# Rows of the first three chunks gathered ahead of the branch, in a graph network kernel on one core

## The chip, the core and the metric

The kernel runs on one core of a Trainium2 chip. The metric is the device time of one execution in microseconds, as the median over several runs. A core has five engines with instruction streams of their own, each of which runs in order: PE (matrix products and transposes), DVE (element-wise work and reductions), ACT (activations and copies), POOL (here almost only the issue of indirect transfers) and SP (here only the issue of plain transfers). PEld stands for PE's loading of its fixed operand. Transfers between the chip's memory and the on-chip buffers are done by 16 DMA engines.

## What is computed

Two graph attention layers with a batch normalisation between them, over 6250 nodes of 128 features and 106,250 edges that are sorted by target node, then a residual and a layer normalisation. Cut to what matters:

```python
def _transformer_conv(h, edge_attr, src, dst, Wq, bq, Wk, bk, Wv, bv, We, Ws, bs):
    q, k, v = ...                        # h @ W + b, as (n, H=2, 64)
    e = (edge_attr @ We).reshape(-1, H, C)
    kj = k[src] + e
    alpha = jnp.einsum('ehc,ehc->eh', q[dst], kj) / sqrt(C)
    a = ...                              # softmax of alpha over the edges of one dst
    out = segment_sum((v[src] + e) * a[:, :, None], dst, num_segments=n)
    return out.reshape(n, H * C) + h @ Ws + bs

rel_t = last_update[src] - t             # node_vec[src] - edge_weight
edge_attr = concatenate([cos(rel_t[:, None] * time_w + time_b), msg], -1)   # 32 + 64 columns
h = _transformer_conv(x, edge_attr, ...)
h = relu(batchnorm(h))
out = layernorm(x + _transformer_conv(h, edge_attr, ...))
```

For each edge the features of its source node are needed, in the first layer also one number of that node, its time, from which 32 cosines of the edge are made.

## The kernel before, in words

**The plan.** The first part (L1429 to L1607) runs ahead of a branch. It loads the sources, the targets and the weights of the edges as 104 rows of 1024 and turns them into columns (`columns`: `fsrcs` at the start, `fdsts` later, `few`, the edge weights, as the last thing): 8 columns of 128 edges for each of 104 chunks. It loads `x` in four parts into `fhT`, where node times stand beside the rows as column 0 (the copies of L530), and writes this 129-column form back to memory as `xv_d`. It checks that the edges are as the fast path wants them and leaves the verdict in `oki`. It makes the matrices of the first layer (`matrices`: L583 to L604), a code matrix (`codes`: L614 to L622), and the first 512 nodes' block of a table that the scores are read from (`tables`: L630 to L642, with a skip row block). PE's results go through two rings of two PSUM banks, `fpt` (128 columns) and `fpx` (512 columns). Each engine then loads `oki` and branches, to `ordered`, or else to `general`, which is not run here.

**The fast path.** `ordered` turns the features of all nodes into columns (`turn_features`: L656 and L658, twelve groups of four transposes, whose copies alternate between DVE and ACT, and a short one, L661 and L662) and then runs `conv(0)` and `conv(1)`. Each goes over 104 chunks of 1024 edges in rounds written out by hand: in round k chunk k is scored (`score`, L954), the weights of chunk k-1 are turned (`turn_weights`, L978), chunk k+1 is turned (`turn_in`: the gathered rows by L913, the encoded edge terms by L925), chunk k+2's times become cosines (`encode`: the angle on DVE, L878 to L886, and the sine on ACT, L892), the bits of chunk k+3's targets are made (`mark`: L829 to L832), chunk k+4 is fetched, and chunk k-1's weighted rows are summed (`gather_sums`, L1001).

**The gathers.** The 1024 source rows of a chunk come by eight indirect transfers of 128 rows each, issued by POOL (`gather`, L839), in the first layer from `xv_d`, in the second from `h_d` and `hn_d`. A chunk's edge data, rows and times share one tile `ff`, from a pool of 7 in the first layer and of 6 in the second. A chunk is gathered four rounds ahead in the first layer and three in the second. Tile 0 of chunk k+4 follows the last step of an earlier `gather_sums`, tile 1 the first half of `score(k)`, tile 2 the turned weights of chunk k-1, tile 3 `finish_turn`, tiles 4 and 5 the two halves of `turn_in(k+1)`, tiles 6 and 7 the first and second third of `gather_sums(k-1)`. These are waits of POOL for PE. Rounds -4 to -2 only fetch and gather chunks 0 to 2, without such waits; chunk 3 belongs to round -1.

**The extra work.** A generator `rest()` supplies work that isn't tied to a chunk, a step at each pull, a few pulls at the end of a round: in before first `targets()` (L712 to L738, PE at L732), which gives the sums of a round their target rows, then the other blocks of the table (L630, L638), then the second layer's matrices.

The early rounds pull two steps each:

```python
pull(extra, (3 if k == 3 else 2) if c and k < 6 else 2 if k < 4 or k > 96 else 1)
```

## Time and profile before

| What | Value |
|---|---|
| Median of three runs | 2177.34 us (2177.1, 2177.34 and 2183.26) |
| Profiled execution | 2178.58 us, of which the recorded span is 2176.8 us |
| Mean granted clock of PE | 0.874 |
| Busy: PE, DVE, ACT, POOL | 1664.4, 1104.6, 972.6, 1578.6 us |
| First gather, last gather of conv 0, first of conv 1 | 33.59, 1072.41, 1106.24 us |
| Branch on PE | between 43.5 and 44.5 us |

A row of the timeline gives the start, the duration, the engine and line, what is written and read, the number of instructions put together, and in brackets how long the engine had been idle and what ended that. "issue" there means that nothing in the profile was waited for. A row of groups gives total busy time, mean time of one in ns, idle time before them and the releaser. A row of windows gives busy time in a stretch, with the clock granted to PE, the share of the DMA engines' time and GB/s at the end. Line numbers are those of the kernel before, and `f` is put in front of the tiles' names.

### The profile page before, as it was taken

Reading aid. Unit: us, or ns where it says so; the run is one execution under the profiler, and the core shown is the slowest. Engines: PE = TensorE matmul, PEld = TensorE weight load, DVE = VectorE, ACT = ScalarE, POOL = GpSimd, SP = SyncE. Lnnn points to the kernel's source line nnn. Section 1 sums busy time; section 2 is a strip of 40 time slices with the busy share of each in tenths; the row PEclk is TensorE's granted clock in tenths of the full one; section 3 lists DMA queues with packets and bytes.
Section 4 is the critical chain, followed back from the end, with each engine's and each line's share of the span. In section 5 each row is a group of like instructions: output and inputs, shape, how many; then the busy total and the mean of one; then the engine's idle time right before and its main releaser. Section 6 shows DMA issues by size and latency. Waiting matters only on the chain.

```text
span 2176.8 us, 46498 instructions
## 1 busy us (share of the span) xinstructions
PE 1664.4 (76%) x13227; PEld 984.3 (45%) x13227; DVE 1104.6 (51%) x3702; ACT 972.6 (45%) x1828; POOL 1578.6 (73%) x1684
## 2 busy tenths in 40 slices
PE   5887787877777878877867777787877778786776
PEld 3455455545455545554534434443444434443333
DVE  4866666656666666676636333333333333332223
ACT  1766666655555555566643333333332333332223
POOL 3777777777777777777557777777777777777773
PEclk9889988879999999899888888888888888888888
DMA  7777777777677777778758667676666667677662
GB/s 210 197 224 210 206 221 211 212 202 210 191 213 199 212 213 210 205 215 219 214 156 240 190 170 193 180 197 178 185 193 188 193 182 187 181 196 185 172 157 76
DMA packets 427316, 424.02 MB, mean 195 GB/s; under 512 B 297704, under 2 KB 344722, under 8 KB 423722
## 3 DMA queue, kind: packets, MB, share of 16 engines
q1 hardware_dynamic: 353086, 272.62, 44.0%
q0 software_dynamic: 53184, 109.45, 21.0%
q10 hardware_dynamic: 20780, 38.87, 5.0%
q8 instruction: 109, 1.79, 0.4%
q14 instruction: 157, 1.29, 0.2%
HBM read 274.73 MB, written 142.58 MB: 192 GB/s over the span
## 4 chain that ended last, share of the span: by engine, by line
DMA 36%; PE 34%; DVE 15%; issue 8%; POOL 4%; ACT 2%; SPq 1%; DVEq 0%; POOLq 0%; ACTq 0%
DMA ff<-hn_d,fsrcs 19%; DMA ff<-xv_d,fsrcs 11%; PE fpa L1001 9%; PE fps L954 7%; PE fpx L913 5%; POOL ff L839 4%; DVE farg L885 3%; PE fpg L630 3%; PE fpe L925 2%; PE fpa L1025 1%; DVE fa L1013 1%; PE fppt L978 1%; DVE fangles L883 1%; DVE farg L879 1%; DVE fangles L882 1%
## 5 line engine op out<-in xcount | busy, mean ns | idle before, releaser
L839 POOL DMA_INDIRECT ff<-xv_d,fsrcs x831 | 786.8, 947 | 283.1 <-issue 115.5
L839 POOL DMA_INDIRECT ff<-hn_d,fsrcs x783 | 742.5, 948 | 241.1 <-issue 105.4
L913 PE MATMUL fpx<-fident,ff 128*128 128x128 f32 x1664 | 335.8, 312 | 231.1 <-DMA ff<-hn_d,fsrcs 211.2
L1001 PE MATMUL fpa<-ff,fpt 128*32 128x256 f32 (+1 forms) x4160 | 416.2, 453 | 0.5 <-ACT fpt L979 0.4
L917 ACT COPY fft<-fpx 128x512 f32<-128x512 f32 x404 | 234.6, 581 | 354.1 <-PE fpx L913 348.8
L913 PEld LDWEIGHTS fpx<-fident,ff 128*128 128x128 f32 x1664 | 229.8, 156 | 294.8 <-DMA ff<-hn_d,fsrcs 248.8
L979 ACT COPY fpt<-fppt 128x384 f32<-128x384 f32 x208 | 99.9, 480 | 504.8 <-PE fppt L978 477.8
L954 PE MATMUL fps<-fft,ftab 128*32 128x384 f32 (+2 forms) x1782 | 264.8, 514 | 32.6 <-ACT fs L969 31.1
L1001 PEld LDWEIGHTS fpa<-ff,fpt 128*32 128x32 f32 (+1 forms) x4160 | 143.7, 129 | 272.2 <-issue 188.5
L1084 DVE TENSOR_SCALAR fout<-fres,fmean,fvar 64x128 f32<-64x128 f32 x104 | 36.7, 353 | 348.2 <-ACT fvar L1082 340.2
L1025 PE MATMUL fpa<-fsel,fa 128*128 128x128 f32 x207 | 65.1, 315 | 160.3 <-DVE fsel L1015 153.4
L925 PE MATMUL fpe<-fident,ff 128*112 128x128 f32 x832 | 153.3, 317 | 3.0 <-ACT ff L892 3.0
L962 DVE TENSOR_REDUCE flow<-fps 128x1 f32<-128x384 f32 x208 | 115.4, 555 | 77.0 <-PE fps L954 75.3
L878 DVE TENSOR_TENSOR frel<-ff,few 128x8 f32<-128x8 f32 (+1 forms) x105 | 18.2, 174 | 254.8 <-DMA ff<-xv_d,fsrcs 254.4
L926 ACT COPY fet<-fpe 112x512 f32<-112x512 f32 x208 | 123.6, 595 | 47.1 <-DMA et_d<-fet 34.1
L954 PE MATMUL fps<-fet,ftab 112*32 112x384 f32 (+3 forms) x968 | 143.0, 456 | 0.0
L885 DVE SCALAR_TENSOR_TENSOR farg<-fangles,farg 128x256 f32<-128x256 f32 (+1 forms) x315 | 132.8, 421 | 10.9
L978 PE MATMUL fppt<-fident,fs 128*128 128x128 f32 x626 | 111.7, 289 | 28.5 <-DVE fbits L829 16.7
L954 PEld LDWEIGHTS fps<-fft,ftab 128*32 128x32 f32 x1782 | 86.3, 119 | 96.4 <-ACT fs L969 44.5
L969 ACT ACTIVATE fs<-fps,fm 128x384 f32<-128x384 f32 x208 | 121.2, 583 | 7.9 <-DVE fm L964 6.9
L954 PE MATMUL fps<-fxT,ftab 112*32 112x384 f32 (+2 forms) x900 | 120.6, 492 | 3.2 <-DMA fxT<-et_d 3.0
L925 PEld LDWEIGHTS fpe<-fident,ff 128*112 128x112 f32 x832 | 120.2, 158 | 3.9 <-ACT ff L892 3.9
(247 smaller groups left out, 2421.3 us busy)
## 6 DMA issues: line engine op xcount, KB each, us to landing
ea_d<-ff SPq DMA_DIRECT2D x104, 448.0 KB
et_d<-fet SPq DMA_DIRECT2D x104, 448.0 KB
ff<-ea_d SPq DMA_DIRECT2D x104, 448.0 KB
fxT<-et_d SPq DMA_DIRECT2D x104, 448.0 KB
tab_d<-fo ACTq DMA_DIRECT2D x26, 1024.0 KB
ftab<-tab_d SPq DMA_DIRECT2D x832, 32.0 KB
ff<-in_edge_attr SPq DMA_DIRECT2D x103, 256.0 KB
ff<-xv_d,fsrcs POOLq DMA_INDIRECT x831
```

What stands on the lines that cost most here:

```text
L839: row = nc.gpsimd.indirect_dma_start(out=f[:, t, :D + 1 - c], out_offset=None, in_=(h_d[:N, :] if k < RAW else hn_d) if c else pl.xv_d, in ...
L885: nc.vector.scalar_tensor_tensor(arg, turn, -part, arg, op0=OP.mult, op1=OP.add)
L913: last = nc.tensor.transpose(px[:, t * P:(t + 1) * P], s.x[:, u * 4 + t, 1 - c:1 - c + D], ident)
L917: nc.scalar.copy(s.ft[:, u * GE:(u + 1) * GE], px)
L925: last = nc.tensor.transpose(pe[:EC, t * P:(t + 1) * P], s.e[:, u * 4 + t], ident)
L926: nc.scalar.copy(s.et[:, u * GE:(u + 1) * GE], pe[:EC])
L954: steps.append(nc.tensor.matmul(s.ps[r, to:to + n], s.tab[:kd, r, i], (ets if i else fts)[:kd, at:at + n], start=i == 0, stop=i == 1 and t ...
L962: nc.vector.tensor_reduce(low, s.ps, AX.X, OP.min)
L969: nc.scalar.activation(s.s[:, :s.ps.shape[1]], s.ps, AF.Exp, bias=s.bias, scale=-1.0)
L978: last = nc.tensor.transpose(pp[:, t * P:(t + 1) * P], s.s[:, t * P:(t + 1) * P], ident)
L979: nc.scalar.copy(s.pt[:, :n * P].rearrange("p (g t c) -> p t g c", g=NQ, c=GH), pp[:, :n * P].rearrange("p (t g c) -> p t g c", g=NQ, c=GH))
L1001: steps.append(nc.tensor.matmul(s.pa[g * GH:(g + of) * GH].rearrange("p (a d) -> p a d", a=2), s.pt[:, (g * n + t) * GH:(g * n + t + of) * ...
```

## The change

Five things change together.

1. The chunks' buffers become one tile, `fring`, of seven slots, allocated ahead of the plan and used by both layers (`split_rows`); `general` uses the same room.
2. The 24 gathers of chunks 0 to 2 move into the plan, behind the column of sources. They read rows of 128 columns from `x` itself and leave the time column free; `gather` returns at once for these chunks.
3. The time column of these chunks is filled by `pick_times`: for each half chunk (six units) one product spreads the high part of the source numbers over 49 partitions, a comparison makes a 0/1 matrix of it, four products with the times (`fhours`, 49 x 128) pick a row of 128 times for each edge, and four reductions with an equality on the low part pick one of them. The units are interleaved with `matrices` and `tables`.
4. `turn_features` leaves the place ahead of conv 0 and becomes the first part of `rest()`, ahead of `targets()`: four groups are pulled in round -1, five in round 0, and in round 1 the last three, the short one and `targets()`.
5. `hide()` in the second layer takes its buffers in turn from two pools.

```diff
+RING = 7
+EARLY = 3
...
+def split_rows(pl, slot):
+    f = pl.ring[:, slot % RING]
+    return (f, f[:, :T * EC].rearrange("p (t d) -> p t d", d=EC),
+            f[:, T * EC:].rearrange("p (t d) -> p t d", d=1 + D))
+
+def pick_times(nc, pl, pool, bank, srows, node_vec):
...
+    for k in range(EARLY):
+        times = split_rows(pl, k)[2]
+        for u in range(T // 4):
+            pb = bank()
+            nc.tensor.matmul(pb[:NA], one[:, k], hi[:, u * GE:(u + 1) * GE], start=True, stop=True)
+            oh = pool.tile([NA, GE], F32, name="foh", bufs=2)
+            nc.vector.tensor_scalar(oh, pb[:NA], lane[:NA], None, op0=OP.is_equal)
+            yield
+            pc = bank().rearrange("p (i n) -> p i n", n=P)
+            for i in range(4):
+                nc.tensor.matmul(pc[:, i], oh[:, i * P:(i + 1) * P], pl.hours, start=True, stop=True)
+            for i in range(4):
+                t = u * 4 + i
+                junk = pool.tile([P, P], F32, name="fjunk", bufs=2)
+                nc.vector.scalar_tensor_tensor(junk, pl.place_of, lo[:, t, k:k + 1], pc[:, i], op0=OP.is_equal,
+                                               op1=OP.mult, accum_out=times[:, t, 0:1])
+            yield
...
-            s.f = load.tile([P, T * FW], F32, name="ff")
...
+            s.f, s.e, s.x = split_rows(pl, k + c * NC)
...
         def gather(k, rows, behind=None):
             f = ch[k].x
+            if c == 0 and k < EARLY:
+                return
...
-                step = put_rows(hn_d, b0, *turned_rows(b0, small.tile([P, GE // P, P], F32, name="fhn", bufs=4)))
+                rows = small.tile([P, GE // P, P], F32, name="fhn", bufs=2) if b0 % 2 else None
+                step = put_rows(hn_d, b0, *turned_rows(b0, rows))
...
+                if c == 0 and k in (-1, 0, 1):
+                    pull(extra, 4 if k < 0 else 2)
...
-                        pull(extra, (3 if k == 3 else 2) if c and k < 6 else 2 if k < 4 or k > 96 else 1)
+                        pull(extra, (3 if k == 3 else 2) if c and k < 6 else 1 if k < 0 else 3 if k < 4 else 2 if k == 4 or k > 96 else 1)
...
-            turn_features(nc, pl, mp, N)
...
             others = second()
+            yield from turn_features(nc, pl, lambda: pl.bank(), N)
             targets()
...
+        nc.sync.dma_start(got.hours[:N // P], node_vec[:N // P * P].rearrange("(a b) -> a b", b=P))
+        nc.sync.dma_start(got.hours[N // P:, :N % P], node_vec[N // P * P:].rearrange("(a b) -> a b", a=1))
...
         columns(srows, srcs)
+        for k in range(EARLY):
+            to = split_rows(got, k)[2]
+            for t in range(T):
+                nc.gpsimd.indirect_dma_start(out=to[:, t, 1:], out_offset=None, in_=x,
+                                             in_offset=bass.IndirectOffsetOnAxis(ap=srcs[:, t, k:k + 1], axis=0))
...
+        hours = pick_times(nc, got, pl, wide, srows, node_vec)
         for _ in matrices(nc, got, 0, keep, bank, pl):
-            pass
+            next(hours, None)
...
         for _ in tables(nc, got, 0, xT0, 0, mw, wide):
+            next(hours, None)
+        for _ in hours:
             pass
         columns(erows, ew)
```

What the change does to the order of instructions stands here at three places; names with DMASW, DMAHW, PE or DVE in brackets are semaphores that are waited for, of software-issued and hardware-issued transfers and of engines.

POOL around the branch (L1610 and L1668 load the check's result, L839 and L883 are the line of `gather`). Before:

```order
19 L1610 TENSOR_LOAD oki [waits DVE_49]
20 L1611 COMPARE_AND_BRANCH
21 L839 DMA ff<-xv_d,fsrcs 128x129 [waits DMAHW5_49,DMAHW3_49,DMAHW7_49,DMAHW0_49,DVE_49]
22 L839 DMA ff<-xv_d,fsrcs 128x129 x3
23 L839 DMA ff<-xv_d,fsrcs 128x129 [waits DVE_49]
```

After, rows 20 to 39 being the 24 gathers from `x`, of which the last stands here:

```order
39 L1576 DMA fring<-in_x,fsrcs 128x128 [waits DMASW7_49]
40 L1668 TENSOR_LOAD oki [waits DVE_49]
41 L1669 COMPARE_AND_BRANCH
42 L883 DMA fring<-xv_d,fsrcs 128x129 [waits DMAHW5_49,DMAHW2_49,DMAHW7_49,DMAHW1_49,DMASW0_49]
43 L883 DMA fring<-xv_d,fsrcs 128x129 [waits DMASW1_49]
44 L883 DMA fring<-xv_d,fsrcs 128x129 [waits DMASW2_49]
45 L883 DMA fring<-xv_d,fsrcs 128x129 [waits DMASW3_49]
46 L883 DMA fring<-xv_d,fsrcs 128x129 [waits DMASW4_49,PE_49]
47 L883 DMA fring<-xv_d,fsrcs 128x129 [waits DMASW5_49,PE_49]
```

The gathers of chunks 0 to 2 have moved ahead of the branch, and the first one behind it is chunk 3's, whose tiles 4 and 5 (rows 46 and 47) wait for PE as they did.

PE from the first table product to the branch (L630 are table and skip products, L1519 and L1569 the columns of edge weights). Before:

```order
19 L630 MATMUL fpx<-fxT_318,fm_273 128x512
20 L630 MATMUL fpx<-fxT_318,fm_281 128x512
21 L630 MATMUL fpx<-fxT_318,fm_289 128x512
22 L630 MATMUL fpx<-fxT_318,fm_297 128x512
23 L630 MATMUL fpx<-fxT_318,fws_107 128x512
24 L1519 MATMUL fpx<-fident,erows 128x104 x8
25 L1610 TENSOR_LOAD oki
```

After (L694 spreads the high parts, L700 picks the rows of times):

```order
25 L630 MATMUL fpx<-fxT_410,fm_331 128x512
26 L694 MATMUL fpx<-fhif,fone 49x512
27 L630 MATMUL fpx<-fxT_410,fm_343 128x512
28 L700 MATMUL fpx<-fhours,foh 128x128 x4
29 L630 MATMUL fpx<-fxT_410,fm_364 128x512
30 L694 MATMUL fpx<-fhif,fone 49x512
31 L630 MATMUL fpx<-fxT_410,fm_376 128x512
32 L700 MATMUL fpx<-fhours,foh 128x128 x4
33 L630 MATMUL fpx<-fxT_410,fws_112 128x512
34 L694 MATMUL fpx<-fhif,fone 49x512
35 L700 MATMUL fpx<-fhours,foh 128x128 x4
36 L1569 MATMUL fpx<-fident,erows 128x104 x8
```

Half of the six units lie here, between and behind the table's products and ahead of the edge weights' columns; the other half lies among the matrices before.

PE in the first rounds, from the branch on (L656 turns features; L913 and L925 before, L958 and L970 after, turn a chunk; L954 and L999 score). Before:

```order
26 L1611 COMPARE_AND_BRANCH
27 L656 MATMUL fpx<-fident,fhT 128x128 x48
28 L661 MATMUL fpx<-fident,fxrest 128x128
29 L913 MATMUL fpx<-fident,ff 128x128 x4
30 L925 MATMUL fpe<-fident,ff 112x128 x4
```

After, with the targets' products (L776) and the first sums (L1046) at the end of the piece:

```order
58 L958 MATMUL fpx<-fident,fring 128x128 x4
59 L970 MATMUL fpe<-fident,fring 112x128 x4
60 L958 MATMUL fpx<-fident,fring 128x128 x4
61 L970 MATMUL fpe<-fident,fring 112x128 x4
62 L656 MATMUL fpg<-fident,fhT 128x128 x12
63 L662 MATMUL fpg<-fident,fxrest 128x128
64 L776 MATMUL fpg<-faway,pones 32x104 x12
65 L1046 MATMUL fpa<-fring,fpt 32x256 x12
```

The 48 transposes that stood ahead of chunk 0 now stand behind it in three pieces, of 16, 20 and 12, and the targets' products, which stood between the scores of chunks 0 and 1, stand between the score of chunk 1 and the first sums.

More of the change, by code (lines that the diff above doesn't have):

```diff
@@ L70, in general @@
 def general(ctx: ExitStack, tc: tile.TileContext, x, src, dst, edge_attr_64, edge_weight, node_vec,
-            time_w, time_b, conv1, conv2, bn_g, bn_b, out):
+            time_w, time_b, conv1, conv2, bn_g, bn_b, out, room):
     nc = tc.nc
@@ L129, in general @@
     nc.sync.dma_start(ew, edge_weight.rearrange("(p j) -> p j", j=EC))
-    xall = const.tile([P, NB, D], F32, name="xall")
+    xall, skip = (room[:, i * NB * D:(i + 1) * NB * D].rearrange("p (b d) -> p b d", d=D) for i in range(2))
     if NR:
@@ L233, in general @@
         nc.vector.tensor_copy(pos, posf)
-    skip = const.tile([P, NB, D], F32, name="skip")
     def project(c, b0, n, hT, kv_d, qt_d, work, psum):
@@ L643, in tables, with turn_features @@
         yield
-def turn_features(nc, pl, mp, N):
+def turn_features(nc, pl, bank, N):
     xT = pl.xT
@@ L653, in turn_features @@
         n = min(4, NF - b0)
-        px = mp.tile([P, 4, P], F32, name="fpx")
+        px = bank().rearrange("p (i n) -> p i n", n=P)
         for i in range(n):
@@ L1276, in ordered @@
     with tc.tile_pool(name="fpw", bufs=2) as pw:
-        with tc.tile_pool(name="ftp", bufs=3, space=bass.MemoryType.PSUM) as mp, tc.manual_schedule():
-            turn_features(nc, pl, mp, N)
         def pass_rows(b0):
@@ L1450, in tile_gnn_resnorm @@
         got.times = keep.tile([P, N // P], F32, name="fnv")
+        got.ring = keep.tile([P, RING, T * FW], F32, name="fring")
+        got.hours = pl.tile([-(-N // P), P], F32, name="fhours")
+        nc.gpsimd.memset(got.hours[32:], 0.0)
         got.raw, got.web, got.ws, got.mats = {}, {}, {}, ([], [])
@@ L1613, in tile_gnn_resnorm @@
     with tc.If(ok < 1):
-        general(tc, x, src, dst, edge_attr_64, edge_weight, node_vec, time_w, time_b, conv1, conv2, bn_g, bn_b, out)
+        general(tc, x, src, dst, edge_attr_64, edge_weight, node_vec, time_w, time_b, conv1, conv2, bn_g, bn_b, out,
+                got.ring.rearrange("p k w -> p (k w)"))
 _PRE = "L0_gnn_"
```

21 lines of the change are left out of this document (18 added, 3 removed).

## The prediction

> **What bounds the kernel now.** I read the page first, for the busiest engine, then POOL's timeline from end to end, then the timelines of PE and DVE from the plan to the first rounds, which is where every edit lies. The page's rows for POOL and for the row gathers:
>
> ```profile
> PE 1664.4 (76%) x13227; PEld 984.3 (45%) x13227; DVE 1104.6 (51%) x3702; ACT 972.6 (45%) x1828; POOL 1578.6 (73%) x1684
> ...
> L839 POOL DMA_INDIRECT ff<-xv_d,fsrcs x831 | 786.8, 947 | 283.1 <-issue 115.5
> L839 POOL DMA_INDIRECT ff<-hn_d,fsrcs x783 | 742.5, 948 | 241.1 <-issue 105.4
> ```
>
> Nearly all of POOL's work is gathers of 0.95 us each. 73% busy looks like room; POOL's timeline shows that there is none (start, duration, engine, line, idle before it and what ended that):
>
> ```profile
> 33.59 1.11 POOL L839 DMA_INDIRECT ff<-xv_d,fsrcs  x1 [30.17 <-DMA fwv<-in_L_gnn_Wv]
> ...
> 63.70 0.94 POOL L839 DMA_INDIRECT ff<-xv_d,fsrcs  x1 [0.30 <-issue]
> ...
> 69.94 0.94 POOL L839 DMA_INDIRECT ff<-xv_d,fsrcs  x1 [0.30 <-issue]
> ...
> 91.41 0.94 POOL L839 DMA_INDIRECT ff<-xv_d,fsrcs  x1 [0.30 <-issue]
> ...
> 1072.41 0.94 POOL L839 DMA_INDIRECT ff<-xv_d,fsrcs  x1 [0.30 <-issue]
> 1106.24 0.94 POOL L839 DMA_INDIRECT ff<-h_d,fsrcs  x1 [32.89 <-DVE fshift L1367]
> ...
> 1112.85 0.94 POOL L839 DMA_INDIRECT ff<-h_d,fsrcs  x1 [0.68 <-PE fpg L630]
> ```
>
> From the first gather of conv 0 to its last lie 830 steps in 1072.41 - 33.59 = 1038.8 us, 1.25 us a step: 0.94 and an idle 0.30 that no wait lengthens. The stream never stops, so the end of conv 0 is its start plus its steps, and whatever delays one gather delays all behind it. So the change is judged by one thing: how many microseconds earlier or later this stream runs after its last disturbed gather. Counting from 33.59, gather 24 (chunk 3, tile 0) is the row at 63.70, gather 29 (chunk 3, tile 5) that at 69.94, gather 46 (chunk 5, tile 6) that at 91.41.
>
> **The early gathers.** They wait only for the column of sources, and POOL has nothing else to do before the branch:
>
> ```profile
> 9.13 1.29 DVE L1520 CAST fsrcs<-fpx 128x416 int32<-128x416 f32 x2 [1.05 <-PE fpx L1519]
> ```
>
> From 10.4, 24 x 1.25 = 30 us bring POOL to 40.4; a load of the check's result and a branch follow, for which I allow 3 us (the branch costs PE 0.4 us at most, below). Chunk 3 could start at 43.5 in place of 63.70: 20 us are on offer. They are had only if nothing that POOL waits for comes late, and in the changed order gathers 28 and 29 wait for PE's turning of the first and second half of chunk 0, and 46 for the first third of the first sums.
>
> **The picked times.** Rows of the plan's end, then the group of row reductions that are nearest to the new picks, and the busy times from the first matrix to the branch:
>
> ```profile
> 33.36 0.69 DVE L1601 COPY fxT<-fpx 128x512 f32<-128x512 f32 x1 [0.56 <-PE fpx L1599]
> 34.10 6.27 PE L630 MATMUL fpx<-fxT,fm 128*128 128x512 f32 x8 [0.79 <-DVE fxT L1601]
> ...
> 43.57 0.59 DVE L1520 COPY few<-fpx 128x416 f32<-128x416 f32 x1 [0.67 <-PE fpx L1519]
> 44.53 1.50 PE L656 MATMUL fpx<-fident,fhT 128*128 128x128 f32 x12 [1.00 <-DVE few L1520]
> 46.97 0.06 DVE L701 MEMSET qpi<- 128x1 f32 x1 [2.81 <-DMA skip_d<-fskip]
> ...
> 48.10 1.01 DVE L658 COPY fxT<-fpx 128x512 f32<-128x512 f32 x1
> ...
> 82.25 1.88 PE L630 MATMUL fpg<-fxT,fm 128*128 128x512 f32 x4
> ```
> ```profile
> L1071 DVE SCALAR_TENSOR_TENSOR fres<-fpa,fr x104: 272/282/284, 1164.0 to 2169.1; 64x128 f32<-64x128 f32 x104
> L1071 DVE DVE_READ_ACCUMULATOR fres<-fpa,fr x104: 73/74/77, 1164.2 to 2169.3; 64x1 f32 x104
> ```
> ```profile
> 25.40:44.20 18.80, 14.91 (x44) 8.33 (x42) 6.50 (x19) 4.62 (x9) 8.17 (x9) 1.00 0.57 193
> ```
>
> (The window row gives PE, weight loads, DVE, ACT and POOL busy, then clock and DMA.) A 512-column product is two records: 6.27 / 4 = 1.57 us here, 1.88 / 2 = 0.94 us at 82.25. Each of the six picking units has 512 columns twice (one product of 512, four of 128): 6 x 2 x 0.94 = 11.3 us of PE if it is fast, 6 x 2 x 1.57 = 18.8 us if slow. On DVE a unit is a comparison of 512 columns (0.69, the copy at 33.36) and four reductions of 0.28 + 0.07: 6 x 2.1 = 12.6 us, and about 2 us ahead of the first unit for indices and lanes (three operations on the 1024-wide rows or the 147-wide one, three small ones). DVE has 18.80 - 6.50 = 12.3 us free in this stretch and PE 3.9, so PE binds, and the units, being PE to DVE to PE to DVE over two banks, leave little of PE's wait to be filled. The last weight column (43.57 + 0.59 = 44.2) then ends at 25.4 + 14.9 + 11.3 = 51.6 at the least, with PE fast and never waiting, and at 25.4 + 18.8 + 18.8 + 2.2 = 65.2 at the most, with every old wait kept, PE slow and the setup in front. I take the old stretch, the mean of the two PE prices (15.0, since in the row at 34.10 about half the records are slow) and 1 us for the half of the setup that the weight transposes don't hide: 25.4 + 18.8 + 15.0 + 1 = 60. All engines pass the branch after that; PE at 44.53 did so within 0.4 us.
>
> The rule of the Trainium skill that bears on this, TensorE: Matmul & The Clock Gate, Part 1 (The HAM clock gate), is that the array runs at half rate by default, goes to full rate after about 3.4 us of sustained work and back after a window of that length without work. The row at 34.10 agrees that one stretch holds both rates, and by the rule as it stands six unbroken units would be fast from the second on (some 12 us of PE, the columns at 57, the forecast 3 us lower), while units broken by waits could stay slow throughout (65, and 5 us higher).
>
> **From the branch to chunk 0 turned.** Rows of the first rounds:
>
> ```profile
> 53.86 0.15 DVE L878 TENSOR_TENSOR frel<-ff,few 128x8 f32<-128x8 f32 x1
> 57.22 1.28 ACT L892 ACT_TABLE_LOAD   x1
> 59.24 0.51 ACT L892 ACTIVATE ff<-farg,qpi 128x256 f32<-128x256 f32 x1 [0.74 <-DVE farg L886]
> 59.75 0.17 DVE L878 TENSOR_TENSOR frel<-ff,few 128x8 f32<-128x8 f32 x1
> 61.55 1.06 PE L925 MATMUL fpe<-fident,ff 128*112 128x128 f32 x4
> 63.17 0.35 DVE L886 TENSOR_SCALAR farg<-farg 128x256 f32<-128x256 f32 x1
> 63.44 0.21 DVE L829 TENSOR_TENSOR fbits<-fdsts,fbitm 128x64 int32<-128x64 int32 x1
> 64.48 0.56 DVE L962 TENSOR_REDUCE flow<-fps 128x1 f32<-128x384 f32 x1 [0.45 <-PE fps L954]
> ```
>
> Before, 9.7 us lie between the columns and the first angle (44.2 to 53.86), most of it turning of features and 2.81 of wait for the skip rows. Both go: the turning stands behind chunk 0, and the skip rows leave a unit before the columns. Left are the small operations, 1.2 us (46.97 to 48.10, and one more), and 0.4 for the branch: the angle starts at 61.6 and takes 3.75 (59.75 to 63.52). The sine's table load, 1.28, ran ahead of the angle and now waits for DVE first, so it counts in full; with the sine's 0.51 and a handover the sine ends at 67.3, and PE finishes turning chunk 0 2.9 us later, as before (59.75 to 62.61): 70.2. Gather 29 starts at 70.5 against 69.94: +0.6 us (28, behind the first half, 1.7 us ahead of it). So the 20 us on offer turn into a wait of POOL in front of these two.
>
> **From there to the first sums.** More rows, of before's targets and sums and of the feature copies:
>
> ```profile
> 69.68 0.13 DVE L712 CAST fhr<-lane_i 128x1 f32<-128x1 int32 x1
> ...
> 73.97 0.79 DVE L728 TENSOR_TENSOR faway<-fpast 1x104 f32<-1x104 f32 x4
> 74.28 1.08 PE L732 MATMUL fpg<-faway,pones 1*32 1x104 f32 x8 [0.34 <-DVE faway L728]
> ...
> 84.06 1.50 PE L1001 MATMUL fpa<-ff,fpt 128*32 128x256 f32 x24
> ...
> 91.62 1.65 PE L1001 MATMUL fpa<-ff,fpt 128*64 128x256 f32 x20
> ```
> ```profile
> L658 DVE COPY fxT<-fpx x6: 1008/1025/1040, 48.1 to 55.6; 128x512 f32<-128x512 f32 x6
> ```
>
> In the new order DVE does, between the first angle and the last step of the targets that PE needs: four angles with their gaps (4 x 3.85 = 15.4), three marks (three operations like that at 63.44, 0.6 each: 1.8), two score minima (the 0.56 at 64.48 and a small step, 0.74 each: 1.5), the six feature copies of 1.02 that are DVE's with the short last one and a clear (6.8), and the targets (69.68 to 74.76: 5.1): 30.6 us. From 61.6 that is 92.2 if DVE never waits. In before it idled 6 us over the same work, and the waits for scores are still there, with PE turning features between them: 0 to 6 us, of which I take 2, because the copies now lie where DVE waited. PE's last target products end 0.6 later (75.36 against 74.76), a third of the sums takes 0.5, the step 0.3: gather 46 at 95.6 against 91.41, +4.2. This is the later of the two gates and sets the stream. After it PE needs 7.6 us a round (84.06 to 91.62) against 10 us for eight gathers, catches up within the lead, and nothing brings the 4 us back or adds to them.
>
> **What costs nothing, or nearly.** One ring of seven in place of pools of seven and six takes no instruction, and 24 gathers of 128 in place of 129 columns cost POOL the same step. In the second conv seven buffers let an edge load start earlier, but the gathers bind there too. At its start the first gather sheds waits of a reopened pool (it stood behind DVE's last shift, 1106.24). But gather 5, at 1112.85, already idles 0.68 in place of 0.30 for a product of the new table, so what is won ahead of it is lost there unless that product comes earlier too: of 0 to 1 us I take 0.2. hide() with half the buffers alternates two tiles; its copies sit in conv 1's rounds, where POOL binds: 0. The two loads of fhours sit ahead of the writes of xv_d on SP's queue; only chunk 3 reads xv_d, and POOL is not there before 43, so 0. The 24 transfers meet the loads of x:
>
> ```profile
> 10.00:15.00 5.00, 2.62 (x16) 1.88 (x16) 1.67 (x13) 0.00 (x0) 0.00 (x0) 1.00 1.10 284
> 15.00:20.00 5.00, 0.32 (x2) 0.00 (x0) 4.52 (x29) 0.00 (x0) 0.00 (x0) 1.00 1.13 323
> ```
> ```profile
> q0 software_dynamic: 53184, 109.45, 21.0%
> ```
> ```profile
> 22.32 0.17 DVE L530 COPY fhT<-fnv 128x12 f32<-128x12 f32 x1
> ```
>
> The DMA share is full from 10 to 20 us. All 1662 gathers take 21.0% of 2176.8 us, 0.275 us of all 16 engines each, so the nine or ten issued by 22.3 take up to 2.6 us from the last part of x, whose copy at 22.32 stands on DVE ahead of the check and the matrices. It had not been waiting; the cost is 0 to 2.6 and I take 0, with 2.6 in the range.
>
> **The sum.** Profiled execution 2178.6 (span 2176.8) + 4.2 - 0.2 = 2182.6. The median shown is 1.24 below that execution, so 2181.
>
> **Rivals.**
> *The gates don't bind (faster).* For it: 20 us lie idle in front of gathers 28 and 29. Every microsecond that the columns end ahead of 60 moves both gates: with the columns at 51.6 and no wait on DVE gather 46 could run at 95.6 - 8.4 - 2.0 = 85.2, -6.2 us: 2171; with no gate at all -20 us: 2157. Against it: six units cannot be had from PE for less than 11.3 us. It decides for faster only if the columns end before about 51.
> *PE slow and DVE waiting (slower).* The columns at 65.2 and 6 us of waits before the sums put gather 46 at 95.6 + 5.2 + 4.0 = 104.8, +13.4 us: 2191. For it: window clocks around the first rounds,
>
> ```profile
> 53.90:84.10 30.20, 20.51 (x130) 11.94 (x132) 23.93 (x77) 17.41 (x25) 22.89 (x25) 0.77 0.74 191
> ```
>
> a granted clock of 0.77 in the very stretch that now holds turned features as well. It decides from gather 46 at about 98 on.
> *The early transfers hold x back.* 2.6 us on top of the forecast: 2184, at the edge of slower.
> *Nothing gained, nothing lost.* The gates fall where gathers 29 and 46 stood, 2177: a part of the forecast's own range.
>
> **How the numbers follow.** About 0.3% (6.5 us) is what a measurement can tell from no change. Forecast, between -6 and +6.5 us: 0.50. First rival beyond -6.5: 0.15. Slow PE: 0.30, x held back: 0.05. So faster 0.15, same 0.50, slower 0.35. The range goes from the first rival's 2171 to the second's 2191.
>
> **What would show it.** POOL: 24 gathers from 10.4 to about 41, then four of chunk 3, an idle of over 15 us in front of the fifth, ended by PE's turning of chunk 0, near 69; shorter waits until gather 46, near 95; no wait after that, and conv 0's last gather near 1076.6. DVE: the columns at 60. PE: the first sums at 95. I am wrong if the columns come at once after the plan's old end, if later rounds still wait for PE, or if conv 1 changes its length.

## The result and the profile after

The changed kernel takes 2199.07 us (median of four runs, 2196.22 to 2201.99) against 2177.82 us for the kernel before: a ratio of 1.0094 with a 95% interval of 1.0082 to 1.0106. It is slower by about 21 us, where no measurable change (2181) was forecast. In the profiled executions the span grew from 2176.8 to 2194.8 us, by 18.0.

First POOL's timeline of the changed kernel, with the same landmarks as in the prediction (L1576 are the early gathers, L883 the others):

```profile
9.81 1.11 POOL L1576 DMA_INDIRECT fring<-in_x,fsrcs  x1 [6.03 <-DVE fsrcs L1570]
...
40.32 0.94 POOL L1576 DMA_INDIRECT fring<-in_x,fsrcs  x1 [0.30 <-issue]
41.57 0.94 POOL L883 DMA_INDIRECT fring<-xv_d,fsrcs  x1 [0.30 <-issue]
...
82.89 0.94 POOL L883 DMA_INDIRECT fring<-xv_d,fsrcs  x1 [36.63 <-PE fpx L958]
84.60 0.94 POOL L883 DMA_INDIRECT fring<-xv_d,fsrcs  x1 [0.77 <-PE fpe L970]
...
110.85 0.94 POOL L883 DMA_INDIRECT fring<-xv_d,fsrcs  x1 [5.27 <-PE fpa L1046]
...
1090.94 1.03 POOL L883 DMA_INDIRECT fring<-xv_d,fsrcs  x1 [0.30 <-issue]
1121.94 0.94 POOL L883 DMA_INDIRECT fring<-h_d,fsrcs  x1 [29.98 <-DMA h_d<-fhr]
...
1130.25 0.94 POOL L883 DMA_INDIRECT fring<-h_d,fsrcs  x1 [2.37 <-PE fpg L630]
```

The 24 early gathers run as planned and chunk 3 starts at 41.57, 22 us earlier than before. Then POOL stands still for 36.6 us in front of gather 28, until PE has turned the first half of chunk 0, and once more for 5.3 us in front of gather 46, which waits for the first sums. That gather starts at 110.85, 19.4 us later than before. From there the stream runs at 1.25 us a step, and the last gather of conv 0 comes at 1090.94, 18.5 us late. So the whole loss was made before 111 us.

The reason stands in PE's timeline in the plan:

```profile
48.90 2.07 PE L630 MATMUL fpx<-fxT,fm 128*128 128x512 f32 x2 [0.78 <-DVE fxT L1657]
50.91 1.94 PE L694 MATMUL fpx<-fhif,fone 3*49 3x512 f32 x2
52.77 2.08 PE L630 MATMUL fpx<-fxT,fm 128*128 128x512 f32 x2
54.78 2.07 PE L700 MATMUL fpx<-fhours,foh 49*128 49x128 f32 x8
56.78 2.07 PE L630 MATMUL fpx<-fxT,fm 128*128 128x512 f32 x2
...
69.44 2.07 PE L700 MATMUL fpx<-fhours,foh 49*128 49x128 f32 x8 [0.84 <-DVE foh L696]
71.44 0.95 PE L1569 MATMUL fpx<-fident,erows 104*128 104x104 f32 x4
```

Every 512-column product takes 1.9 to 2.0 us from start to start, from the first to the last, the table's own products (L630) as well. The groups of those table products, of the kernel before and of the changed one (shortest, median and longest record in ns; a product is two records):

```profile
L630 PE MATMUL fpx<-fxT,fm x8: 592/1061/1221, 34.1 to 39.8; 128*128 128x512 f32 x8
```
```profile
L630 PE MATMUL fpx<-fxT,fm x8: 1057/1140/1222, 48.9 to 61.7; 128*128 128x512 f32 x8
```

Before, six records of 1.0 to 1.2 us were followed by two of 0.6, some 5 us into the stretch. After, none became short, though PE hardly paused: the window row of that stretch shows 23.29 us of PE busy in 24.50.

```profile
49.00:73.50 24.50, 23.29 (x48) 9.71 (x48) 8.46 (x30) 3.01 (x3) 0.00 (x0) 1.00 0.16 60
```

The granted clock in it reads 1.00 (the first of the last three columns), but that is no measurement. The trace lists the granted clock in stretches of 0.5 and of 1.0; the list begins with the first change, and the window view counts what lies ahead of it as 1.00. In the kernel before, the first full stretch begins at 39.31 us, between the last slow record (start 38.53) and the first fast one (39.35). In the changed kernel it begins at 84.73 us. So PE ran at half clock through the whole plan, as the records' durations say too.

Half clock alone makes a product of 512 columns last 1.71 us from start to start (53.11 to 54.82 in the timeline of f1_full below; in the kernel before the slow records stand 0.85 apart, two to a product). The rest, up to 0.3 us, belongs to the change of shape between neighbours: in the changed kernel the weights of a product with other rows or columns are loaded only as that product starts (50.90), while in f1_full, an experiment below in which all these products have 128 rows and columns, they are loaded 0.85 us ahead of it (52.26 for the product at 53.11):

```profile
50.90 0.24 PEld L694 LDWEIGHTS fpx<-fhif,fone 3*49 3x49 f32 x2 [1.50 <-issue]
```
```profile
52.26 0.34 PEld L694 LDWEIGHTS fpx<-fhif,fone 128*128 128x128 f32 x1 [0.52 <-issue]
```

The last weight column therefore ended at 74.35 and not at 60:

```profile
73.76 0.59 DVE L1570 COPY few<-fpx 128x416 f32<-128x416 f32 x1 [0.54 <-PE fpx L1569]
```

### The profile page after: what moved, and what is told of

Its sections match the earlier page's. It is cut to its first block, busy times and chain, and to the rows that moved or that the text cites. A ratio compares the mean times of both kernels' runs of the same rounds, so it can differ in the third digit from the quotient of the medians.

```text
span 2194.8 us, 45383 instructions
## 1 busy us (share of the span) xinstructions
PE 1669.1 (76%) x13287; PEld 981.7 (45%) x13287; DVE 1118.7 (51%) x3762; ACT 969.9 (44%) x1828; POOL 1579.2 (72%) x1685
## 4 chain that ended last, share of the span: by engine, by line
DMA 33%; PE 33%; DVE 15%; issue 9%; POOL 5%; ACT 3%; SPq 1%; DVEq 0%; POOLq 0%; ACTq 0%
DMA fring<-hn_d,fsrcs 19%; DMA fring<-xv_d,fsrcs 9%; PE fpa L1046 9%; PE fps L999 7%; POOL fring L883 5%; PE fpx L958 5%; DVE farg L930 3%; PE fpg L630 3%; DMA et_d<-fet 2%; PE fpe L970 2%; DVE fa L1058 1%; PE fpa L1070 1%; DVE farg L924 1%; DVE farg L925 1%; DVE fangles L927 1%
## 5 line engine op out<-in xcount | busy, mean ns | idle before, releaser
L883 POOL DMA_INDIRECT fring<-xv_d,fsrcs x807 | 762.8, 945 | 287.9 <-issue 104.0
L883 POOL DMA_INDIRECT fring<-hn_d,fsrcs x783 | 742.1, 948 | 240.3 <-issue 111.6
L958 PE MATMUL fpx<-fident,fring 128*128 128x128 f32 x1664 | 325.7, 306 | 234.7 <-DMA fring<-hn_d,fsrcs 214.7
L1046 PE MATMUL fpa<-fring,fpt 128*32 128x256 f32 (+1 forms) x4160 | 414.6, 453 | 0.5 <-ACT fpt L1024 0.4
L958 PEld LDWEIGHTS fpx<-fident,fring 128*128 128x128 f32 x1664 | 222.5, 152 | 296.0 <-DMA fring<-hn_d,fsrcs 251.3
L999 PE MATMUL fps<-fft,ftab 128*32 128x384 f32 (+2 forms) x1782 | 267.6, 518 | 48.7 <-ACT fs L1014 47.5
L1046 PEld LDWEIGHTS fpa<-fring,fpt 128*32 128x32 f32 (+1 forms) x4160 | 143.6, 129 | 267.3 <-issue 178.6
L970 PE MATMUL fpe<-fident,fring 128*112 128x128 f32 x832 | 146.8, 307 | 6.4 <-ACT fring L937 6.0
L999 PE MATMUL fps<-fet,ftab 112*32 112x384 f32 (+3 forms) x968 | 145.1, 460 | 0.0
L923 DVE TENSOR_TENSOR frel<-fring,few 128x8 f32<-128x8 f32 (+1 forms) x105 | 18.2, 174 | 239.8 <-DMA fring<-xv_d,fsrcs 239.2
L999 PEld LDWEIGHTS fps<-fft,ftab 128*32 128x32 f32 x1782 | 86.0, 118 | 111.6 <-ACT fs L1014 63.2
L999 PE MATMUL fps<-fxT,ftab 112*32 112x384 f32 (+2 forms) x900 | 120.5, 492 | 3.4 <-DMA fxT<-et_d 3.2
L970 PEld LDWEIGHTS fpe<-fident,fring 128*112 128x112 f32 x832 | 115.0, 153 | 7.7 <-ACT fring L937 7.1
```

Source lines behind the costliest of these rows:

```text
L883: row = nc.gpsimd.indirect_dma_start(out=f[:, t, :D + 1 - c], out_offset=None, in_=(h_d[:N, :] if k < RAW else hn_d) if c else pl.xv_d, in ...
L958: last = nc.tensor.transpose(px[:, t * P:(t + 1) * P], s.x[:, u * 4 + t, 1 - c:1 - c + D], ident)
L970: last = nc.tensor.transpose(pe[:EC, t * P:(t + 1) * P], s.e[:, u * 4 + t], ident)
L999: steps.append(nc.tensor.matmul(s.ps[r, to:to + n], s.tab[:kd, r, i], (ets if i else fts)[:kd, at:at + n], start=i == 0, stop=i == 1 and t ...
L1046: steps.append(nc.tensor.matmul(s.pa[g * GH:(g + of) * GH].rearrange("p (a d) -> p a d", a=2), s.pt[:, (g * n + t) * GH:(g * n + t + of) * ...
```

## The experiments

**Theory A** was that PE stays slow in the plan because the picking products use few of the array's 128 rows (3 in the spreading product, 49 in the picking one), and that everything after follows the weight columns at a fixed distance. **Theory B** was that the alternation of products, comparisons and waits keeps PE slow, whatever the rows. A second question was whether early gathers, ring and moved features cost something by themselves.

The first four kernels (e1 to e4) ran on a chip on which the kernel before takes 2647 us. What makes that chip slower isn't known; the profiles of one and the same kernel, e4_early0 there and h2_early0 elsewhere, show the same busy time of POOL (1580.5 and 1577.6 us) and longer waits, 1024 us in place of 571 in front of the gathers. So the times of e1 to e4 compare only among themselves, and all four kernels were measured again, as f1_full, f3_nopick, f4_times and h2_early0.

**e1_full and f1_full: products filled up with zeros.** Rows and columns are filled, `fhours` likewise to 128 rows; the order stays, and the comparison on DVE covers 128 partitions in place of 49.

```diff
-    hi = pool.tile([EARLY, CE], F32, name="fhif")
+    hi = pl.hi                       # [128, CE], zeros from a memset by POOL at the start
...
-    one = pool.tile([EARLY, EARLY, NA], F32, name="fone")
+    one = pool.tile([P, EARLY, P], F32, name="fone")
...
-            nc.tensor.matmul(pb[:NA], one[:, k], ...)
-            oh = pool.tile([NA, GE], F32, name="foh", bufs=2)
+            nc.tensor.matmul(pb, one[:, k], ...)
+            oh = pool.tile([P, GE], F32, name="foh", bufs=2)
```

> The picking products are filled up with zeros to 128 rows and 128 columns (3 x 49 and 49 x 128 in the changed kernel); their order, number, width and waits stay. Theory A, PE's clock stays low in the plan because these products use few of the array's rows: the 512-column records fall from 1.06 to about 0.59 us some 5 us into the dense stretch that begins at 48.9 (or earlier), the columns of edge weights end at 55 to 64 in place of 74.3, and the time falls by 10 to 18 us, to 2181 to 2189. Theory B, the clock stays low because products and comparisons alternate with waits, whatever the rows: records stay at 1.06, columns at 74, time 2199.

> The picking products filled up with zeros to 128 rows and 128 columns once more, since in the run before every engine waited longer for its instructions and for the others (the kernel before took 2647 us there), which hides what the plan does to the time. Theory A (rows of the array in use decide PE's clock): in the stretch of table products and picks the 512-column products fall from 2.0 to 1.0 us after some 4 us, the columns end near 62, gather 46 at 98 to 99, time 2185 to 2189. Theory B (alternation and waits decide): products stay at 2.0 us, columns at 74, time 2199.

e1_full took 2658.93 us against 2646.86 (1.0047, 1.0031 to 1.0063). f1_full, where the kernel before took 2178.44, took 2191.27 (1.0061, 1.0044 to 1.0078). PE's timeline of f1_full:

```profile
36.40 2.08 PE L694 MATMUL fpx<-fhif,fone 128*128 128x512 f32 x2
38.40 0.79 PE L598 MATMUL fpt<-ftr,ftr 64*128 64x128 f32 x2
38.99 0.42 PE L602 MATMUL fpt<-fbq,ftr 64*128 64x1 f32 x2
39.34 2.08 PE L700 MATMUL fpx<-fhours,foh 128*128 128x128 f32 x8
...
51.24 2.08 PE L630 MATMUL fpx<-fxT,fm 128*128 128x512 f32 x2 [0.78 <-DVE fxT L1659]
53.11 1.91 PE L694 MATMUL fpx<-fhif,fone 128*128 128x512 f32 x2
54.82 1.36 PE L630 MATMUL fpx<-fxT,fm 128*128 128x512 f32 x2
56.02 1.05 PE L700 MATMUL fpx<-fhours,foh 128*128 128x128 f32 x8
57.45 1.12 PE L630 MATMUL fpx<-fxT,fm 128*128 128x512 f32 x2 [0.38 <-ACT fo L636]
```

Same order, same number of products, same partners: from 51.24 on the products fall to half some 4 us into the stretch, and the trace's first stretch of full clock begins at 55.49. Theory B falls. The columns ended at 68.7, 5.6 us earlier than in the changed kernel although this plan starts about 1 us later (POOL's clearing of the padded tile); 62 had been expected. The rest is the first half of the plan, 30 to 47 us, which stays slow here too (the first four rows): there the filled products alternate with products of 64 rows and of one column. PE was busy for all of the 11 us from 34 to 45, so idle gaps are hardly the reason; whether the 64 rows are, or the one column, was not tried.

**f2_spread, g2_cols, g3_rows: which filling counts.** f2 fills only the spreading product in both ways, g2 only its columns, g3 only its rows; the picking product keeps 49 rows in all three.

```diff
 # g2_cols
-    one = pool.tile([EARLY, EARLY, NA], F32, name="fone")
+    one = pool.tile([EARLY, EARLY, P], F32, name="fone")
 # g3_rows, with hi = pl.hi as above
+    one = pool.tile([P, EARLY, NA], F32, name="fone")
```

> Only the spreading products (3 x 49 in the changed kernel) are filled up to 128 x 128; the picking products keep 49 rows. Theory A, graded: the mean of rows in use over the stretch lies between the two others, so the clock rises later or not at all; if it rises as in f1_full the 3-row products alone held it down (columns near 62, time 2185 to 2189), if not 49 rows are too few as well (columns at 74, 2199). Theory B: 2199.

> The spreading product keeps its 3 rows and gets 128 columns of weights in place of 49; all else as in the changed kernel. If the rows in use decide PE's clock: products stay at 2.0 us in the whole plan, columns at 74, time 2199. If the product of rows and columns, or the columns, decide: products fall to 1.0 us some 4 us into the dense stretch, columns at 68 to 69, time 2191.

> The spreading product gets 128 rows (125 of them zero) and keeps its 49 columns; all else as in the changed kernel. If the rows in use decide PE's clock: products fall to 1.0 us some 4 us into the dense stretch, columns at 68 to 69, time 2191. If rows and columns must both be filled: 2.0 us throughout, columns at 74, time 2199.

f2_spread took 2191.52 us (1.0063, 1.0046 to 1.0080), g2_cols 2201.22 (1.0104, 1.0084 to 1.0124), g3_rows 2193.61 (1.0069, 1.0049 to 1.0089), the last two from two executions each. The spreading product's records in g2_cols, then in g3_rows:

```profile
L694 PE MATMUL fpx<-fhif,fone x12: 1052/1122/1217, 30.1 to 69.1; 3*128 3x512 f32 x12
```
```profile
L694 PE MATMUL fpx<-fhif,fone x12: 592/1057/1090, 31.0 to 63.8; 128*49 128x512 f32 x12
```

With 3 rows no record becomes fast, with 128 rows (125 of them zeros) they do, and the columns of weights don't matter for it. The trace's list of the granted clock says the same: the first full stretch begins at 55.49, 55.27 and 55.84 us in f1_full, f2_spread and g3_rows, and at 84.73, 88.40 and 84.46, behind the plan, in the changed kernel, g2_cols and h1_featback (below), which keep the 3 rows. The change of shape between neighbours is not the reason, since f2_spread and g3_rows have it too. So of theory A the 3 rows hold and the 49 don't: a 3-row product in every fourth place, beside one of 49 rows in another, keeps PE slow, and 49 rows beside 128 do not. Where between 3 and 128 the line lies isn't shown.

**e2_nopick, f3_nopick and g1_nopick: no picks.** The time column of chunks 0 to 2 is set to zero. In e2 and f3 (the same kernel) DVE sets it where the picks began, in g1 POOL sets it ahead of the first gather.

```diff
-        hours = pick_times(nc, got, pl, wide, srows, node_vec)
+        for k in range(EARLY):       # e2, f3; in g1 by POOL behind the ring's allocation
+            nc.vector.memset(split_rows(got, k)[2][:, :, 0:1], 0.0)
```

> The picking of times is left out (the time column of chunks 0 to 2 is set to zero, so the cosines of these chunks are other numbers); early gathers, ring and moved features stay. Theory A, the picks alone push the columns and everything follows the columns by a fixed distance (gather 46 came 36.5 us after the columns): columns at 45 to 46, gather 46 near 82, 9 us ahead of the kernel before, time about 2168. Rival, the moved features and targets hold gather 46 back by themselves: gather 46 near 91 or later, time 2177 or more.

> The picks left out once more (time column of chunks 0 to 2 zero, so the cosines of these chunks are other numbers). Theory A: columns at 45 to 46, gather 46 at 82, 9 us ahead of the kernel before, time about 2168. Rival (moved features and targets hold gather 46 by themselves): 2177 or more.

> The picks left out (time column of chunks 0 to 2 zero), now set by POOL before the first gather: in f3_nopick DVE's clearing of those columns waited for the rows to land, 14.9 us ahead of the matrices, so the columns of edge weights ended at 59.4 there. Theory A (everything follows the columns): columns at 45 to 46, gather 46 at 37 to 38 us behind them, 82 to 84, 7.5 to 9 us ahead of the kernel before; time 2168 to 2171. Rival: gather 46 near 91 or more, time 2177 or more.

e2_nopick: 2644.32 us (0.9993, 0.9978 to 1.0008). f3_nopick: 2185.99 us (1.0034, 1.0020 to 1.0047), a miss: expected was 2168. DVE's timeline of f3_nopick shows why:

```profile
35.41 0.07 DVE L1646 MEMSET fring<- 128x8 f32 x1 [8.08 <-DMA fring<-in_x,fsrcs]
42.17 0.07 DVE L1646 MEMSET fring<- 128x8 f32 x1 [6.70 <-DMA fring<-in_x,fsrcs]
```

The clearing, one strided operation over all eight tiles of a chunk, waited for the rows of that chunk to land, so the experiment had put a new wait of 14.8 us ahead of the matrices. It still fits the second half of theory A: columns at 59.8, gather 46 at 97.87, span 2183.7. In g1_nopick that wait is gone: 2173.93 us, ratio 0.9978 (0.9968 to 0.9987), faster than the kernel before, 3 us above what was expected. Gather 46 came at 85.88, 40.2 us behind the columns and not 37 to 38, and DVE's timeline of g1_nopick names the difference:

```profile
45.11 0.59 DVE L1568 COPY few<-fpx 128x416 f32<-128x416 f32 x1 [0.67 <-PE fpx L1567]
49.56 0.06 DVE L745 MEMSET qpi<- 128x1 f32 x1 [3.86 <-DMA ftab<-tab_d]
```

Without a pick unit between the skip rows and the columns a wait at the branch is back (2.81 us in the kernel before, ended by the skip rows; 3.86 here, ended by the table; 0.54 in the changed kernel).

**e3_times and f4_times: one chunk early, its times by transfers.** One chunk, EARLY = 1, no picks; the times are gathered too.

```diff
-EARLY = 3
+EARLY = 1
...
+            for t in range(T):
+                nc.gpsimd.indirect_dma_start(out=to[:, t, 0:1], out_offset=None,
+                                             in_=node_vec.rearrange("(n a) -> n a", a=1),
+                                             in_offset=bass.IndirectOffsetOnAxis(ap=srcs[:, t, k:k + 1], axis=0))
```

> One chunk in place of three is gathered ahead of the branch, and its times come by eight more indirect transfers of 128 single numbers straight from node_vec, no picks. POOL has 23 us idle between the sources (9.8) and the first gather behind the branch (33.6 in the kernel before), 16 transfers of 1.25 us take 20 of them. Theory A (stream and columns): chunk 1 starts at 33.6 in place of 43.6, columns at 45, gather 46 at 82 at the latest, 9 to 10 us earlier: about 2168. Rival, transfers of single numbers take longer on POOL or land late, or the first gathers wait: 2177 or more.

> One chunk gathered ahead of the branch, its times by eight transfers of single numbers, no picks. Theory A: chunk 1 at 33.6 to 35, columns at 45, gather 46 at 81 to 83, time about 2168 (2171 if the first gather behind the branch waits for the copy of x until 35). Rival (times land late or a later wait takes over): 2177 or more.

e3_times: 2634.52 us (0.9959, 0.9947 to 0.9970). f4_times: 2172.54 us (0.9973, 0.9963 to 0.9984), about 6 us faster than the kernel before and 26 us under the changed one: it beats both. It is 1.5 us above the upper value that was expected. POOL's timeline of f4_times:

```profile
11.63 0.94 POOL L1572 DMA_INDIRECT fring<-in_x,fsrcs  x1 [0.31 <-issue]
...
20.59 0.94 POOL L1575 DMA_INDIRECT fring<-in_node_vec,fsrcs  x1 [0.30 <-issue]
...
29.82 0.94 POOL L1575 DMA_INDIRECT fring<-in_node_vec,fsrcs  x1 [0.31 <-DMA xv_d<-fhT]
34.43 0.94 POOL L883 DMA_INDIRECT fring<-xv_d,fsrcs  x1 [3.67 <-DMA xv_d<-fhT]
...
84.92 0.94 POOL L883 DMA_INDIRECT fring<-xv_d,fsrcs  x1 [3.25 <-PE fpa L1046]
```

The eight gathers of times (L1575) run from 20.59 to 30.76, ahead of the branch. Chunk 1 starts at 34.43, about where chunk 0 used to, and not at 43.74; of the 9.3 us so won the wait in front of gather 46 gives back 3 (84.92, expected 81 to 83).

**e4_early0 and h2_early0: no early gathers, no picks.** EARLY = 0; ring, moved features and targets stay.

> No early gathers and no picks: left of the change are the ring, the moved features and targets, and the two pools in hide. Theory A: POOL's stream starts at 33.6 as in the kernel before, the sums that gather 46 waits for come at 81 and bind nothing: 2176 to 2178, less up to 2 us at the start of the second layer, where the changed kernel's gap between the layers was 31.0 in place of 33.8 us. Rival, the moved features cost by themselves (PE, DVE and ACT busier in rounds 0 and 1): gather 46 beyond 91.4, time above 2179.

> No early gathers and no picks, on a chip whose kernel before takes 2177 us: left are the ring, the moved features and targets, and the two pools in hide. POOL's stream starts at 33.6 to 35, the sums that gather 46 waits for come at 82 to 86 and bind nothing: 2175 to 2179. Rival, the moved features cost by themselves: gather 46 beyond 92, time above 2180.

e4_early0: 2647.57 us (1.0006, 0.9993 to 1.0020). h2_early0: 2180.32 us (1.0005, 0.9993 to 1.0018). The moved work and the ring change nothing that can be measured. By the letter the rival's marks were met, 2180.32 against "above 2180" and gather 46 at 93.42 against "beyond 92". But the ratio can't be told from 1, and POOL's stream had started at 35.30 in place of 33.59, so 1.7 of the 2.0 us at gather 46 were there before it. The first sums started at 89.78, later than expected, but gather 46 ran behind them with the usual 0.30 us:

```profile
93.42 0.94 POOL L883 DMA_INDIRECT fring<-xv_d,fsrcs  x1 [0.30 <-issue]
```

**h1_featback: features and targets back in their old place**, with early gathers and picks.

```diff
-            yield from turn_features(nc, pl, lambda: pl.bank(), N)
+        # ahead of conv 0, as before; the pulls as before
```

> The changed kernel with the feature turning and the targets put back where the kernel before has them (ahead of chunk 0, and at the end of round 0); early gathers and picks stay. If the move takes time out of the way to the first sums (columns to gather 46: 36.5 us in the changed kernel, 47 in the kernel before, of which about 6 are POOL's own stream): columns at 74, gather 46 at 114 to 117, time 2203 to 2206. Rival, the move itself costs (copies of DVE and ACT in rounds 0 and 1): gather 46 at 110 or less, time 2198 or less.

2199.16 us (1.0088, 1.0071 to 1.0105), not to be told from the changed kernel, where 2203 to 2206, or by the rival 2198 or less, had been expected. In the profile gather 46 stood at 113.99 against 110.85, and it waited no more: now chunk 0's turning alone set the stream (gather 28).

```profile
89.84 0.94 POOL L883 DMA_INDIRECT fring<-xv_d,fsrcs  x1 [42.93 <-PE fpx L958]
...
113.99 0.94 POOL L883 DMA_INDIRECT fring<-xv_d,fsrcs  x1 [0.30 <-issue]
```

So the move takes at most some 3 us off gather 46, which the times don't resolve.

**g4_best: f4_times with the first sums earlier.** Targets in round 0, features spread over rounds -1 to 3.

```diff
+        if b0 == 16 and between is not None:
+            between()                # targets()
+            yield
...
+ 2 if k == 0 else 3 if k == 1 else 6 if k == 2 else 5 if k == 3 else 2 if k == 4 or k > 96 else 1)
```

> As f4_times (one chunk early, its times by transfers of single numbers), with the targets pulled in round 0 and the last third of the feature turning behind the first sums. In f4_times gather 46 waited 3.25 us for these sums. Theory A: 2 to 3 us fewer of DVE's copies stand ahead of the sums, gather 46 waits 0 to 1 us, time 2 to 3 us under f4_times: 2169 where that was 2172.5, a ratio to the kernel before of 0.996. Rival: the table's second block, now made in round 3 in one piece, holds a later round back by as much, ratio 0.997 or more.

2178.80 us (0.9999, 0.9989 to 1.0008): the rival's mark was met, and by more than it said. Gather 46 still waits, 1.78 us in place of 3.25, and comes at 84.28 in place of 84.92. But the sums of round 2, behind the features, their copies and a first product of the table that are packed into that round, stop POOL for 7.38 us, eight gathers later and a round earlier than the rival had it:

```profile
101.33 0.94 POOL L886 DMA_INDIRECT fring<-xv_d,fsrcs  x1 [7.38 <-PE fpa L1049]
```

The chain from the columns to the end, over all profiled executions on chips whose kernel before takes 2178 us (times in us; columns are the end of the last weight column):

| Kernel | Columns | Gather 46 | Last gather of conv 0 | Span |
|---|---|---|---|---|
| before | 44.2 | 91.41 | 1072.41 | 2176.8 |
| h2_early0 | 44.5 | 93.42 | 1073.21 | 2177.1 |
| g4_best | 44.4 | 84.28 | 1071.74 | 2174.6 |
| f4_times | 45.1 | 84.92 | 1065.07 | 2166.3 |
| g1_nopick | 45.7 | 85.88 | 1066.72 | 2172.3 |
| f3_nopick | 59.8 | 97.87 | 1078.21 | 2183.7 |
| f2_spread | 68.6 | 105.10 | 1085.55 | 2190.0 |
| f1_full | 68.7 | 105.08 | 1085.49 | 2190.5 |
| g3_rows | 68.8 | 105.16 | 1087.56 | 2193.0 |
| after | 74.4 | 110.85 | 1090.94 | 2194.8 |
| h1_featback | 75.0 | 113.99 | 1094.18 | 2198.7 |
| g2_cols | 75.9 | 112.88 | 1096.25 | 2201.9 |

With early gathers and moved features gather 46 comes 36.4 to 40.2 us behind the columns. The last gather of conv 0 comes 980 to 983 us behind gather 46 in every row but that of g4_best, where the wait of 7.38 us is added. Without early gathers (before, h2_early0) the columns don't set gather 46; there POOL's own stream does. The second layer adds its own scatter of a few us to the spans.

## Why the prediction was wrong

**The bound and the measure: right.** POOL's stream decided. It was 19.4 us late at gather 46, 18.5 at the end of conv 0, and the span 18.0.

**The early gathers: right.** Predicted from 10.4 to 40.4 with chunk 3 at 43.5; measured from 9.81 with chunk 3 at 41.57. The branch cost POOL nothing that shows. The 20 us on offer turned into a wait in front of gather 28, as said, only that the wait grew to 36.6.

**The picked times: the step that failed.** "I take the old stretch, the mean of the two PE prices (15.0, ...) and 1 us": columns at 60, at most 65.2; measured 74.35. The working took 6.27 / 4 = 1.57 us as the price of a slow product. That row was itself a mixture, six slow records and two fast ones, and not half and half as the working says; two slow records in it take 1.71 us. Beside neighbours of another shape a slow product takes 1.9 to 2.0, a cost that the working didn't have. So the mean was a mean with a mean, and the upper end was no upper end. It also let the table's own products keep their old price, though they share PE's clock with what is put between them. The 30.2 us from 44.2 to 74.35 add up from the traces: 23.0 for the six units (6 x 1.9 twice, 15.0 predicted), 2.2 of PE's wait for the setup (1 predicted), 2.7 because five table products took 10.0 and not 7.4, 0.8 for the edge columns at 0.95 in place of 0.57 each, 1.1 by which the plan started later, 0.4 of other waits.

**The rule of the clock gate.** The Trainium skill, TensorE: Matmul & The Clock Gate, Part 1 (The HAM clock gate), has full rate after about 3.4 us of sustained work. The prediction had it make the time 3 us shorter for unbroken units and 5 longer for units broken by waits. The trace doesn't agree: here 23.29 us of busy PE in 24.50 brought no full rate, while the same stretch with 128 rows in the spreading product had it after some 4 us. That an instruction runs is not enough to count as work here; with 3 of 128 rows in every fourth product it did not count enough. The slow PE had been a rival, with 2191 as its price. The rival was right that PE would be slow, and priced 8 us too low for the reasons above; it named the rounds behind the branch for its evidence, while the runs show the plan and the 3 rows.

**From the columns to gather 46: right.** Predicted 35.6 us (60 to 95.6), measured 36.5. The sine's table load now stood behind DVE, and the wait for the skip rows had gone. That the distance came out within 1 us is in part luck, since two errors inside go opposite ways: DVE reached the targets' last step 0.4 us earlier than worked out, while the first sums took 2.6 us and not 1.5, at a clock that stood at 0.5 from 101.80 to 112.04.

**The early transfers against the loads of x.** Taken as 0 of 0 to 2.6; DVE's first cast of targets, which waits for their load, came at 13.20 and not at 12.18, 1.0 us later, and the plan kept that delay. That the early transfers caused it is likely and not shown: without them it came at 12.12 (h2_early0), with one chunk's at 13.02 (f4_times) and 11.80 (g4_best).

**The start of the second layer.** Taken as 0.2; the gap between the layers fell from 33.8 to 31.0 us, of which gather 5's wait took back most, 2.37 in place of 0.68. The stream was 1.1 us less late behind it (1130.25 against 1112.85, 17.4 late, where it had been 18.5 late).

## What to carry to other kernels

Put a price on PE work by the shortest and the longest record of its kind, never by a row that adds several, and ask what clock PE will have with the new neighbours: an old instruction's price can change too. Where small products stand between large ones in a part that waits for PE, fill their contraction up to 128 rows with zeros: PE's records got no longer by it (1.9 us a slow product with 3 rows and with 128), and it returned 5 us of time with the rows alone (g3_rows) and 8 with rows and columns in both products (f1_full), although clearing the padded tile made the plan start 1 to 2 us later. When an engine has idle time before a branch, the fill should be work of that engine (eight more transfers on POOL) rather than work that goes through the engines which the branch waits for.

## What the runs showed of the hardware

PE's clock depends on how many rows its products use: with products of 3 and of 49 rows between 128-row ones PE stayed at 1.9 to 2.0 us for each 512 columns for 25 us, and the trace's first full clock came at 84.73 us; with the 3 rows filled up by zeros it came to about 1.1 us (records of 592 ns) some 4 us into the same stretch, with the first full clock at 55.84 (g3_rows). Filling the columns of the weights (49 to 128) did nothing for it (88.40 in g2_cols). All clocks that the traces list are 0.5 or 1.0. The weights of a product whose rows or columns differ from its neighbour's were loaded only at its own start, 0.3 us of a product of 2.0 at half clock.

A gather of 128 single numbers costs POOL the same step, about 1.25 us, as one of 128 rows of 512 bytes: both took 0.94 us and 0.3 us to the next in the timeline of f4_times (L1575 beside L1572).
